# Routing of two expert layers moved into the per-batch chains, with a staggered write stage, in a four-layer transformer kernel

## The chip, the core and the metric

The kernel runs on one core of a Trainium2 chip. The engines named here are PE (matrix products, with PEld for its weight loads), DVE (vector operations), ACT (activations), POOL (GpSimd, which also issues the indirect transfers) and SP (which issues most plain transfers). DMA transfers go through queues of SP, ACT and POOL. The metric is the device time of one execution in microseconds (us).

## The reference, cut to what matters

Four layers, each a cross-attention and a feed-forward part with experts, on x of 4 batches x 512 tokens x 128 features. What the change touches is how tokens are assigned to expert slots in layers 0 and 2:

```python
# layer 0: one expert for each token, 8 experts, 128 slots each
logits = x @ w_switch + b_switch
routes = softmax(logits).argmax(-1)
oh = one_hot(routes)
pos = (cumsum(oh, axis=0) * oh).sum(-1) - 1
keep = pos < capacity                      # 128
buf[routes * capacity + pos] = x           # tokens kept
y = relu(buf_e @ w1 + b1) @ w2 + b2
out = where(keep, y[slot], x)

# layer 2: two experts for each token, 8 experts, 640 slots each
topv, topi = top_k(x @ w_g, 2)
mask = one_hot(topi.T)                     # all first choices, then all second
rank = cumsum(mask.reshape(2 * N, 8), axis=0) - 1
mask = mask * (rank < capacity)            # 640
# each kept (token, choice): gelu(x @ c_fc[e]) @ c_proj[e], weighted and summed
```

Slots are handed out in the order of tokens, first choices of all tokens before second choices. Which slot a token has does not show in the output; whether it has one does. Layer 1 has 16 experts on 16 soft slots a batch, between a "read" attention (slots look at tokens) and a "write" attention (tokens look at slots). Layer 3 computes all 8 experts on all tokens.

## The kernel before

Tokens lie in tiles of 128; a batch is four tiles (`NJ` = 4, `NT` = 16 in all), and X[g] holds batch g's rows. Work on a batch is written as a generator, a chain, that yields between its parts. `together(chains, skew)` (line 110) advances all running chains by one part in turn; chain i starts i x skew rounds late, and with skew 0 all go in lockstep. `queue` joins generators one after another. This gives the program order; a scheduler then fixes the order on each engine, and an engine works strictly in it.

The stages in order of time in the profile: layer 0's attention with the logits of `routed` (to about 140 us), layer 0's routing and experts in `l0_ffn` (to 184), layer 1's attention and read stage (to 252), layer 1's experts (to 276), the write stage with layer 2's attention and logits (to 341), layer 2's routing (to 357) and experts (to 460) in `l2_ffn`, layer 3's attention and gate (to 546), layer 3's experts (to the end).

Routing before is one block for all 2048 tokens, after the last batch's logits. `argmax` (line 579) finds the first largest logit as a one-hot tile of 128 x 128 (16 tiles x 8 experts); `without` (593) masks it for the second choice. `places` (597) counts tokens of each expert and tile with a product against ones (603), copies the counts on ACT (605), and adds a product with a triangle (608, ranks within a tile) to one with the counts of earlier tiles (611) and, for second choices, those of all first choices (610); `own` and `rank` (613 to 616) pick each token's rank. `tokens_of_slots` (620) turns ranks into a table from slots to tokens: rank modulo 128 as a one-hot 128 x 128 block `R` per tile (637), chunk number and token number in `th` (648), one product for each tile summed in PSUM (652), and a few small operations to `inv` (which token row to gather) and `to` (which row to scatter to). All of them are on DVE, with PE and ACT between.

In layer 0 the eight gathers (`xg`, 680, POOL) and the eight transpositions (712, PE, and copies 713, DVE) are all issued before the first expert. `hidden(e)` (732 to 739) makes the four hidden blocks, with two relus on DVE (737) and two on ACT (739); `outputs` (747, 749) follows for the expert before; each expert's rows are scattered (689, POOL) into `yd`. `combine` (763) reads yd back as `yg`, one transfer of 256 KB a batch on SP, and layer 1 adds it to X (457). Ahead of `l0_ffn` stand eight loads of 512 KB on SP's queue, `e_wg`, one weight of layer 1's experts (`halves`, 1197); the other, `e_w1` (in the profile `e_w`), follows during the experts, and `yg` lies behind its first loads in SP's queue.

The write stage (line 976) runs, for each batch, `write(g)` (block keys, 16-head attention on 16 slots, projection, add to X), then `attend2(g)` and `route2(g)`, the four chains in lockstep. `normed` makes the normalised rows, on DVE (223) or, where `act` is set, on ACT (219). Layer 3's chains and layer 1's read stage run with skew 2 (lines 1134 and 896).

Of the kernel before, what the change touches and what calls it, by code (L numbers as in the profile page):

```python
# [8 lines left out]
F32 = mybir.dt.float32  # L9
# [7 lines left out]
P = 128  # L17
# [28 lines left out]
_CST = [("ident", 128), ("ones", 128), ("tri", 128), ("before", 128), ("same", 128), ("vm8", 64),  # L46
        ("vm16", 32), ("vms", 64), ("hi32", 4), ("hi16", 8), ("selE", 128), ("hm2", 2), ("hm8", 8), ("hm16", 16), ("iota", 128), ("rev", 8),
        ("tile", 2 * NT), ("row", 1), ("spare0", NEXP), ("spare2", NCH2 * NEXP), ("chunks", NCH2), ("ctxT", 128)]
# [19 lines left out]
def tile_kernel(ctx: ExitStack, tc: tile.TileContext, I, out):  # L68
# [8 lines left out]
    rk = ctx.enter_context(tc.tile_pool(name="rk", bufs=1))  # L77

# [83 lines left out]
    for name in ("ones", "tri", "before", "same", "iota", "rev"):  # L162
        exact[name] = const.tile([P, C[name].shape[1]], BF16, tag=f"b_{name}", name=f"b_{name}")
        nc.gpsimd.tensor_copy(exact[name], C[name])
    ones, tri, before, same, iota, rev = exact.values()
# [334 lines left out]
    def l0_xattn(w):  # L500
        every = lambda r: bc(r, 1, NJ)

        def chain(g):
# [20 lines left out]
            hT = [l0.tile([P, S], F32, tag="hT", name="hT", bufs=16) for _ in range(4)]  # L524
# [26 lines left out]
    def routed(tag, w, bias=None, copies=()):  # L551
# [5 lines left out]
        def chain(g):  # L557
            xn[g] = yield from normed(X[g], "xn")
# [20 lines left out]
    def argmax(L, n=NT):  # L579

        m = rt.tile([P, n], F32, tag="m", name="m", bufs=2 * NT // n)
# [4 lines left out]
        w = rt.tile([P, n], F32, tag="w", name="w", bufs=2 * NT // n)  # L586
        nc.vector.tensor_reduce(w, at, AX.X, ALU.max)
        oh = rt.tile([P, n, NEXP], BF16, tag="oh", name="oh", bufs=2 * NT // n)
        nc.vector.tensor_tensor(oh, at, bc(w, 2, NEXP), ALU.is_equal)
        return m, oh  # L590

    def without(L, oh, n=NT):
# [4 lines left out]
    def places(ohs):  # L597

        sums, found = [], []
        for k, oh in enumerate(ohs):  # L600
            oh2 = oh.rearrange("p t e -> p (t e)")
            pt = psum()
            nc.tensor.matmul(pt[:, :P], lhsT=oh2, rhs=ones, start=True, stop=True)
            cs = rt.tile([P, P], BF16, tag="cs", name="cs", bufs=2)
            nc.scalar.copy(cs, pt[:, :P])
            sums.append(cs)
            pt = psum()
            nc.tensor.matmul(pt[:, :P], lhsT=tri, rhs=oh2, start=True, stop=False)
            for k0 in range(k):
                nc.tensor.matmul(pt[:, :P], lhsT=sums[k0], rhs=same, start=False, stop=False)  # L610
            nc.tensor.matmul(pt[:, :P], lhsT=cs, rhs=before, start=False, stop=True)
            own = rt.tile([P, NT, NEXP], F32, tag="own", name="own")
            nc.vector.tensor_tensor(own.rearrange("p t e -> p (t e)"), oh2, pt[:, :P], ALU.mult)
            rank = rt.tile([P, NT], F32, tag="rank", name="rank", bufs=2)
            nc.vector.tensor_reduce(rank, own, AX.X, ALU.add)
            nc.vector.tensor_scalar(rank, rank, -1.0, None, ALU.add)
            found.append(rank)
        return found

    def tokens_of_slots(ohs, ranks, cap, spare):  # L620
# [6 lines left out]
        pt = psum()  # L627
        for k, (oh, rank) in enumerate(zip(ohs, ranks)):
            ri = rt.tile([P, NT], I32, tag="ri", name="ri", bufs=2)
            nc.vector.tensor_copy(ri, rank)  # L630
            nc.vector.tensor_scalar(ri, ri, P - 1, None, ALU.bitwise_and)
            lo = rt.tile([P, NT], BF16, tag="lo", name="lo", bufs=2)
            nc.vector.tensor_copy(lo, ri)
            Rs = []
            for t0 in range(0, NT, NJ):
                R = wk.tile([P, NJ, P], BF16, tag="aT", name="R", bufs=B)
                nc.vector.tensor_tensor(R, bc(iota, 1, NJ), bc(lo[:, t0 : t0 + NJ], 2, P), ALU.is_equal)
                Rs.append(R)
                if t0 == 0:
                    hi = rt.tile([P, NT], F32, tag="hi", name="hi", bufs=2)  # L640
                    nc.vector.tensor_tensor(hi, rank, lo, ALU.subtract)
                    in_ = rt.tile([P, NT, nch], BF16, tag="in", name="in_", bufs=2)
                    nc.vector.tensor_tensor(in_, bc(hi, 2, nch), bc(C["chunks"][:, :nch], 1, NT), ALU.is_equal)
                    tk = rt.tile([P, NT, 2, NEXP], BF16, tag="tk", name="tk", bufs=2)
                    nc.vector.tensor_scalar(tk[:, :, 0, :], oh, C["row"], None, ALU.mult)
                    nc.vector.tensor_tensor(tk[:, :, 1, :], oh, bc(C["tile"][:, k * NT : (k + 1) * NT], 2, NEXP), ALU.mult)
                    th = rt.tile([P, NT, nch, 2 * NEXP], BF16, tag="th", name="th", bufs=2)
                    nc.vector.tensor_tensor(
                        th, bc(tk.rearrange("p t i e -> p t (i e)"), 2, nch), bc(in_, 3, 2 * NEXP), ALU.mult
                    )  # L650
            for t in range(NT):
                nc.tensor.matmul(
                    pt[:, : nch * 2 * NEXP],
                    lhsT=Rs[t // NJ][:, t % NJ, :],
                    rhs=th[:, t].rearrange("p c e -> p (c e)"),
                    start=k == 0 and t == 0,
                    stop=k == len(ohs) - 1 and t == NT - 1,
                )
        inv = rt.tile([P, nch, NEXP], I32, tag="inv", name="inv")
        got = rt.tile([P, nch, 2, NEXP], F32, tag="got", name="got")  # L660
        nc.vector.tensor_copy(got.rearrange("p c i e -> p (c i e)"), pt[:, : nch * 2 * NEXP])
        token = rt.tile([P, nch, NEXP], F32, tag="token", name="token")
        nc.vector.scalar_tensor_tensor(token, got[:, :, 1, :], float(P), got[:, :, 0, :], ALU.mult, ALU.add)
        row = rt.tile([P, nch, NEXP], F32, tag="row", name="row")
        nc.vector.tensor_scalar(row, token, -1.0, 0.0, ALU.add, ALU.max)
        if len(ohs) > 1:
            again = rt.tile([P, nch, NEXP], F32, tag="again", name="again")
            nc.vector.tensor_scalar(again, row, float(NTOK), float(-NTOK), ALU.is_ge, ALU.mult)
            nc.vector.tensor_tensor(inv, row, again, ALU.add)
        else:  # L670
            nc.vector.tensor_copy(inv, row)
        to = rt.tile([P, nch, NEXP], I32, tag="to", name="to")
        none = rt.tile([P, nch, NEXP], F32, tag="none", name="none")
        nc.vector.tensor_scalar(none, token, 0.0, None, ALU.is_equal)
        nc.vector.tensor_tensor(none, none, spare.rearrange("p (c e) -> p c e", c=nch), ALU.mult)
        nc.vector.tensor_tensor(to, row, none, ALU.add)
        return inv, to
# [39 lines left out]
    def l0_ffn(xd, yd, L):  # L717


        _, oh = argmax(L)  # L720
        (rank,) = places([oh])
        inv, to = tokens_of_slots([oh], [rank], L0_CAP, C["spare0"])
        b2 = ex.tile([P, NEXP, D], F32, tag="b2", name="b2")
        nc.scalar.dma_start(b2, I["f0_b2"].partition_broadcast(P))

        xTs = [expert_inputs(fetched(xd, inv, e, 0, 1, NEXP), NEXP) for e in range(NEXP)]

        def hidden(e):
            xT = xTs[e]
# [4 lines left out]
            for f in range(4):  # L734
# [3 lines left out]
                else:  # L738
                    nc.scalar.activation(hT[:, f, :], pt[:, f, :], AF.Relu, bias=b1)
# [96 lines left out]
    def l1_ffn(lw, dq, dv, cq, wg, before, after):  # L836
# [139 lines left out]
        together(queue(write(g), after(g)) for g in range(B))  # L976
# [25 lines left out]
    def l2_ffn(xd, yd, L, f2w1, f2w2, meanwhile):  # L1002
        m1, oh1 = argmax(L)
        m2, oh2 = argmax(without(L, oh1))
        ranks = places([oh1, oh2])

        d = rt.tile([P, NT], F32, tag="d", name="d")
        nc.gpsimd.tensor_tensor(d, m2, m1, ALU.subtract)
        nc.scalar.activation(d, d, AF.Exp)
        inv, to = tokens_of_slots([oh1, oh2], ranks, L2_CAP, C["spare2"])  # L1010
# [92 lines left out]
    def l3_ffn(xnT, logits, f3w1, f3w2, before, fetch):  # L1103
        gates = [None] * B

        def gate(g):
            L = logits[:, g * NJ : (g + 1) * NJ, :]
            m1, oh1 = argmax(L, NJ)
            m2, oh2 = argmax(without(L, oh1, NJ), NJ)
# [64 lines left out]
    for at in range(0, 2 * NTOK, S):  # L1174
        nc.sync.dma_start(yd2[at : at + S].rearrange("(j p) d -> p j d", p=P), zero)
    made = {}
# [229 lines left out]
```

## Time and profile before

| what | us |
| --- | --- |
| median of 14 executions | 677.61 (673.3 to 679.25) |
| the profiled execution, whole | 676.5 |
| its span in the profile | 674.7 |
| last logits of layer 0 to first gather | 140.41 to 149.83 |
| first hidden product of layer 0's experts | 161.66 |
| first rows back, layer 1 starts | 186.61 |
| first score product of the write stage | 276.2 |
| last logits of layer 2 to its first gather | 340.18 to 357.12 |

The granted PE clock was 0.852 over the span. In the views, each line of a timeline has start, duration, engine, line of the kernel, operation, output <- inputs, shape and count, and in brackets the engine's idle time before it with what ended it. Each line of the table by stretches has start:end and length, busy time (and instructions) of PE, PEld, DVE, ACT and POOL, the granted PE clock (1 is full), the mean share of the 16 DMA engines that was busy, and GB/s.

### The profile page before, as it was taken

The page shows a single profiled execution, that of the slowest core. Times are in us where ns is not written, and L with a number is a line of the kernel's source. Part 1 is how long each engine was busy: PE and PEld are TensorE (multiplying, and loading weights), DVE is VectorE, ACT ScalarE, POOL GpSimd, SP SyncE. Part 2 cuts the span into 40 slices and gives each one's busy share as a digit, 9 for nine tenths or more (in the row PEclk, how much of TensorE's full clock was granted, in tenths as well). Part 3 has the DMA queues.
Part 4 walks back from the last instruction along what each step waited for, and adds up shares of the span by engine and source line. Part 5 has one row for each costly group of instructions (what it writes and reads, how often), then busy time and mean ns, then how long its engine had stood idle before and what let it go on. Part 6 is the DMA issues. An engine that isn't in the chain of part 4 may idle for free.

```text
span 674.7 us, 8842 instructions
## 1 busy us (share of the span) xinstructions
PE 516.9 (77%) x3047; PEld 393.6 (58%) x3047; DVE 330.1 (49%) x1378; ACT 239.6 (36%) x539; POOL 163.9 (24%) x203
## 2 busy tenths in 40 slices
PE   3668988426678969787635999951799699999996
PEld 2557765325556543676523887840467557676765
DVE  4686555452377640367781322115767843333322
ACT  2354655300224731324211233221645333333342
POOL 4234234204512100100006777772100000000000
PEclk9979989855855988889675999995799869999999
DMA  9900001281390006300201112354000000000000
GB/s 325 305 29 18 17 16 53 59 309 32 132 291 0 1 0 236 139 2 1 63 1 39 56 52 50 54 175 140 0 1 1 1 0 2 17 0 17 1 17 16
DMA packets 42990, 44.97 MB, mean 67 GB/s; under 512 B 5161, under 2 KB 31026, under 8 KB 42818
## 3 DMA queue, kind: packets, MB, share of 16 engines
q1 hardware_dynamic: 39442, 36.20, 16.2%
q0 software_dynamic: 3072, 6.30, 3.6%
q10 hardware_dynamic: 432, 1.92, 0.7%
q8 instruction: 24, 0.39, 0.3%
q14 instruction: 20, 0.16, 0.1%
HBM read 34.97 MB, written 9.44 MB: 66 GB/s over the span
## 4 chain that ended last, share of the span: by engine, by line
PE 49%; DVE 11%; POOL 5%; DMA 5%; issue 5%; ACT 4%; SPq 1%; POOLq 0%; DVEq 0%; ACTq 0%
PE pt L1146 9%; PE pt L1151 9%; PE pt L1037 4%; PE pt L1045 4%; PE po L404 3%; PE pt L385 3%; POOL yd L689 3%; PE pt L233 3%; PE pt L916 2%; DMA yd<-ye,to 2%; PE pt L398 2%; PE pt L564 2%; POOL xg L680 1%; DVE st L192 1%; PE pt L452 1%
## 5 line engine op out<-in xcount | busy, mean ns | idle before, releaser
L1151 PEld LDWEIGHTS pt<-f3w,hT 128*128 128x128 f32 x512 | 66.1, 192 | 34.0 <-ACT hT L1147 19.0
L1161 DVE SCALAR_TENSOR_TENSOR x<-pt,gates,x 128x128 f32<-128x128 f32 x128 | 36.0, 345 | 84.2 <-PE pt L1151 84.2
L1147 ACT ACTIVATE hT<-pt,cols 128x512 f32<-128x512 f32 x64 | 44.0, 687 | 75.0 <-PE pt L1146 74.7
L1151 PE MATMUL pt<-f3w,hT 128*128 128x128 f32 x512 | 68.6, 277 | 0.9 <-ACT hT L1147 0.6
L1146 PE MATMUL pt<-xnT,f3w 128*128 128x512 f32 x128 | 68.0, 619 | 0.0
L233 PE MATMUL pt<-cst,xn 128*128 128x128 f32 x96 | 25.9, 366 | 42.1 <-ACT xn L219 22.9
L680 POOL DMA_INDIRECT xg<-xd,inv x48 | 46.1, 961 | 44.5 <-DMA e_wg<-in_e_wg 16.4
L1040 ACT ACTIVATE hT<-pt 128x384 f32<-128x384 f32 (+1 forms) x64 | 27.9, 437 | 73.6 <-PE pt L1037 72.1
L689 POOL DMA_INDIRECT yd<-ye,to x48 | 47.0, 979 | 25.6 <-DVE ye L749 13.1
L233 PEld LDWEIGHTS pt<-cst,xn 128*128 128x128 f32 x96 | 15.8, 170 | 53.8 <-ACT xn L219 27.8
L192 DVE BATCH_NORM_STATS2 st<-x 128x6 f32<-128x128 f32 x128 | 32.3, 270 | 23.7 <-POOL x L545 17.6
L1045 PEld LDWEIGHTS pt<-f2w,hT 128*128 128x128 f32 x320 | 39.6, 191 | 3.3
L1045 PE MATMUL pt<-f2w,hT 128*128 128x128 f32 x320 | 40.4, 279 | 0.0
L1037 PE MATMUL pt<-exT,f2w 128*128 128x256 f32 (+1 forms) x128 | 39.1, 449 | 1.0 <-DVE exT L713 1.0
L235 ACT COPY xnT<-pt 128x512 f32<-128x512 f32 x40 | 23.1, 585 | 43.0 <-PE pt L233 42.7
L1052 DVE COPY ye<-pt 128x384 f32<-128x384 f32 (+1 forms) x16 | 7.9, 491 | 57.5 <-PE pt L1045 37.5
L398 PE MATMUL pt<-cst,att 128*128 128x128 f32 x128 | 22.4, 301 | 12.6 <-ACT att L372 12.6
L372 ACT ACTIVATE att<-att 128x512 f32<-128x512 f32 x32 | 20.0, 631 | 27.7 <-DVE att L371 27.6
L1037 PEld LDWEIGHTS pt<-exT,f2w 128*128 128x128 f32 x128 | 23.8, 197 | 9.0 <-DVE exT L713 1.2
L385 PE MATMUL pt<-keys,xnT 128*128 128x256 f32 (+1 forms) x64 | 27.9, 543 | 0.9 <-ACT xnT L235 0.9
L370 DVE TENSOR_REDUCE mx<-pt 128x16 f32<-128x512 f32 (+1 forms) x32 | 21.7, 683 | 12.9 <-PE pt L385 12.7
L404 PEld LDWEIGHTS po<-v,aT 128*128 128x128 f32 x192 | 25.0, 201 | 4.9 <-issue 3.3
(297 smaller groups left out, 1030.5 us busy)
## 6 DMA issues: line engine op xcount, KB each, us to landing
e_wg<-in_e_wg SPq DMA_DIRECT2D x8, 512.0 KB, 7.5
e_w<-in_e_w SPq DMA_DIRECT2D x8, 512.0 KB, 7.1
yg<-yd SPq DMA_DIRECT2D x12, 256.0 KB, 3.6
f0w<-in_f_w SPq DMA_DIRECT2D x1, 2048.0 KB, 13.2
yd<-zero SPq DMA_DIRECT2D x8, 256.0 KB, 3.9
ew<-in_e_w SPq DMA_DIRECT2D x8, 256.0 KB, 3.7
xd<-xn SPq DMA_DIRECT2D x8, 256.0 KB, 2.2
f2w<-in_f_w SPq DMA_DIRECT2D x1, 2048.0 KB, 8.7
```

Of the source, the lines that this page charges most:

```text
L192: nc.vector.bn_stats(st[:p, j, :], src[:, j, :])
L233: nc.tensor.transpose(pt[:, j * P : (j + 1) * P], src[:, j, :], ident)
L385: nc.tensor.matmul(pt[:, j * nk : (j + 1) * nk], lhsT=xT[:, (j0 + j) * P : (j0 + j + 1) * P], rhs=keys, start=True, stop=True,)
L404: nc.tensor.matmul(po[:, k, :], lhsT=aT[:, k * P : (k + 1) * P], rhs=of(values[k % nch], cols + hpc, g), start=True, stop=True,)
L680: nc.gpsimd.indirect_dma_start(out=dst, out_offset=None, in_=table[:], in_offset=bass.IndirectOffsetOnAxis(ap=idx, axis=0))
L689: ins = nc.gpsimd.indirect_dma_start(out=table[:], out_offset=bass.IndirectOffsetOnAxis(ap=to[:, c, e : e + 1], axis=0), in_=y, in_offset=None
L1037: nc.tensor.matmul(pt[:, : m * P], lhsT=f2w1[:, e, f * P : (f + 1) * P], rhs=xT, start=True, stop=True)
L1045: nc.tensor.matmul(pt[:, c * D : (c + 1) * D], lhsT=hT[:, f, c * P : (c + 1) * P], rhs=f2w2[:, e, f, :], start=f == 0, stop=f == 3,)
L1146: nc.tensor.matmul(pt, lhsT=f3w1[:, e, f * P : (f + 1) * P], rhs=xnT[g], start=True, stop=True)
L1147: nc.scalar.activation(hT[:, f, :], pt, AF.Gelu, bias=col["f3_b1"][:, 2 * e + f : 2 * e + f + 1])
L1151: nc.tensor.matmul(pt[:, j, :], lhsT=hT[:, f, j * P : (j + 1) * P], rhs=f3w2[:, e, f, :], start=f == 0, stop=f == 1,)
L1161: nc.vector.scalar_tensor_tensor(xj, pt[:, j, :], ge, xj, ALU.mult, ALU.add)
```

## The change

1. Routing is made per batch. `argmax`, `places` and `tokens_of_slots` give way to `first_max` and `assigned(rt, logits, choices, cap, spare)`. `assigned` returns `chain(g)`, which is queued behind `route0(g)` and `route2(g)`, `finish()`, which makes `inv` and `to` after all batches, and `top`, the largest logits.
2. In the chain, counts of earlier batches are added by products with `same`; the triangle is strict, so that ranks begin at 0. `R` is made by one operation for each tile, comparing a constant row with a column of ranks; the products of each batch are added to a running sum `got`.
3. For layer 2, second choices no longer continue the count of the first. They are counted by themselves and take places from the back of the expert's 640 slots (a reversed row `back` and a reversed table of chunks); where a slot falls to both, the first choice has it.
4. In `l0_ffn`, each expert's transposition and copy stand just before its hidden product, and only its own gather is awaited.
5. The loads `e_wg` move from SP's queue before routing to ACT's queue, issued after the last relu of expert 4.
6. The write stage runs with skew 3. Layer 2's normalised rows are made on ACT (`act=True`).

Buffers move with it: `R` has its own, layer 0's hidden tiles have 12 instead of 16, and the right side of the memory holds `e_wg` and then layer 2's routing tiles.

```diff
-    def routed(tag, w, bias=None, copies=()):
+    def routed(tag, w, bias=None, copies=(), act=False):
...
-            xn[g] = yield from normed(X[g], "xn")
+            xn[g] = yield from normed(X[g], "xn", act=act)
...
+    def assigned(rt, logits, choices, cap, spare):
...
+        def chain(g):
+            oh = rt.tile([P, n, NEXP], BF16, tag="oh", name="oh", bufs=2)
+            L = logits[:, g * NJ : (g + 1) * NJ, :]
+            for k in range(choices):
+                ohk = oh[:, k * NJ : (k + 1) * NJ, :]
+                first_max(rt, top[k][:, g * NJ : (g + 1) * NJ], ohk, L)
+                if k + 1 < choices:
+                    L = without(rt, L, ohk)
+            flat = oh.rearrange("p t e -> p (t e)")
+            pt = psum()
+            nc.tensor.matmul(pt[:width, :P], lhsT=flat, rhs=ones, start=True, stop=True)
+            cs = rt.tile([P, P], BF16, tag=f"cs{g}", name="cs")
+            nc.scalar.copy(cs[:width], pt[:width, :P])
+            counts.append(cs)
...
+            yield
+
+            pt = psum()
+            nc.tensor.matmul(pt[:, :width], lhsT=tri, rhs=flat, start=True, stop=False)
+            for g0 in range(g):
+                nc.tensor.matmul(pt[:, :width], lhsT=counts[g0][:width], rhs=same[:width, :width], start=False, stop=False)
+            nc.tensor.matmul(pt[:, :width], lhsT=cs[:width], rhs=before[:width, :width], start=False, stop=True)
...
+            R = rt.tile([P, n, P], BF16, tag="R", name="R", bufs=2)
+            for t in range(n):
+                nc.vector.tensor_scalar(R[:, t, :], back if t >= NJ else iota, lo[:, t : t + 1], None, ALU.is_equal)
+            yield
...
+            if got:
+                nc.vector.tensor_tensor(flat, pt[:, : choices * m], got[-1].rearrange("p k c i e -> p (k c i e)"), ALU.add)
+            else:
+                nc.vector.tensor_copy(flat, pt[:, : choices * m])
+            got.append(now)
+            yield
...
-        xTs = [expert_inputs(fetched(xd, inv, e, 0, 1, NEXP), NEXP) for e in range(NEXP)]
+        xs = [fetched(xd, inv, e, 0, 1, NEXP) for e in range(NEXP)]
 
         def hidden(e):
-            xT = xTs[e]
+            xT = expert_inputs(xs[e], 3)
...
-                    nc.scalar.activation(hT[:, f, :], pt[:, f, :], AF.Relu, bias=b1)
+                    done = nc.scalar.activation(hT[:, f, :], pt[:, f, :], AF.Relu, bias=b1)
+            if e == NEXP // 2:
+                with tc.issue_after(done.ins):
+                    meanwhile()
...
-        together(queue(write(g), after(g)) for g in range(B))
+        after = then()
+        together([queue(write(g), after(g)) for g in range(B)], 3)
...
-            *(queue(attend0(g), route0(g)) for g in range(B)),
+            *(queue(attend0(g), route0(g), assign0(g)) for g in range(B)),
...
+    slots0 = finish0()
...
-        wg = halves("e_wg", gw, ("wga", "wgb"))
...
+        combine0 = l0_ffn(xd0, yd0, *slots0, lambda: wg.extend(halves("e_wg", gw, ("wga", "wgb"), nc.scalar)))
...
+    route2, _, _, L = routed(2, wide["w_g"], None, (xd2,), act=True)
...
+        return lambda g: queue(attend2(g), route2(g), made["assign2"](g))
```

More of the change, by code (lines that the diff above doesn't have):

```diff
@@ L523, in chain @@
             nc.gpsimd.tensor_tensor(z, z, every(w["rest"][:, 1]), ALU.add)
-            hT = [l0.tile([P, S], F32, tag="hT", name="hT", bufs=16) for _ in range(4)]
+            hT = [l0.tile([P, S], F32, tag="hT", name="hT", bufs=12) for _ in range(4)]
             for f in range(4):
@@ L620, in tokens_of_slots @@
-    def tokens_of_slots(ohs, ranks, cap, spare):
-        nch = cap // P
[L627 to L651, printed above, removed]
-                nc.tensor.matmul(
[L653 to L657, printed above, removed]
-                )
[L659 to L677, printed above, removed]
@@ L834, in l1_ffn_weights, with l1_ffn @@
         return dq, dv, cq
-    def l1_ffn(lw, dq, dv, cq, wg, before, after):
+    def l1_ffn(lw, dq, dv, cq, wg, before, then):
         sc = 1.0 / math.sqrt(8.0)
```

186 lines of the change are left out of this document (118 added, 68 removed).

## The prediction

> **What bounds the kernel now.** I read the page first, then a table of busy time cut at the stages that the change touches, then the timeline inside them, and last the DMA issues.
>
> ```profile
> PE 516.9 (77%) x3047; PEld 393.6 (58%) x3047; DVE 330.1 (49%) x1378; ACT 239.6 (36%) x539; POOL 163.9 (24%) x203
> ```
>
> PE is the busiest engine, but over the whole span. The change touches four stretches only (start:end, length, then busy us of PE, PEld, DVE, ACT and POOL, the granted clock, DMA share, GB/s), with a fifth for comparison:
>
> ```profile
> 133.00:150.00 17.00, 4.73 (x31) 3.41 (x31) 10.25 (x44) 1.26 (x4) 0.58 (x2) 0.50 0.85 308
> 150.00:162.00 12.00, 3.76 (x10) 1.88 (x11) 2.13 (x8) 0.00 (x0) 7.61 (x8) 0.50 0.15 44
> 162.00:184.00 22.00, 17.16 (x128) 16.78 (x127) 7.58 (x25) 5.87 (x16) 7.78 (x8) 0.81 0.28 97
> 276.00:341.00 65.00, 49.48 (x322) 44.37 (x320) 42.47 (x182) 22.59 (x54) 1.64 (x4) 0.82 0.10 31
> 341.00:357.00 16.00, 3.62 (x39) 2.69 (x39) 14.07 (x51) 2.03 (x4) 0.40 (x1) 0.62 0.00 0
> 460.00:546.00 86.00, 63.10 (x345) 46.33 (x346) 66.57 (x306) 36.92 (x85) 5.05 (x4) 0.80 0.09 25
> ```
>
> Line 1 is the end of layer 0's attention and its routing, line 2 the eight gathers and transpositions, line 3 its eight experts, line 4 the write stage with layer 2's attention in lockstep, line 5 layer 2's routing (DVE 14.07 of 16 us, PE nearly idle). Line 6 is layer 3's attention and gate: four chains already staggered, DVE 77% busy.
>
> In layer 0 the timeline gives the marks:
>
> ```profile
> 140.41 0.19 DVE L572 TENSOR_TENSOR logits<-pt,adds 128x32 f32<-128x32 f32 x1 [3.32 <-PE pt L564]
> 148.72 0.17 DVE L671 CAST inv<-row 128x8 int32<-128x8 f32 x1
> 149.83 1.17 POOL L680 DMA_INDIRECT xg<-xd,inv  x1 [16.41 <-DMA e_wg<-in_e_wg]
> 152.83 0.45 PE L712 MATMUL pt<-cst,xg 128*128 128x128 f32 x1 [4.76 <-DMA xg<-xd,inv]
> 161.66 3.64 PE L732 MATMUL pt<-exT,f0w 128*128 128x128 f32 x16
> 174.17 0.37 ACT L739 ACTIVATE hT<-pt,cols 128x128 f32<-128x128 f32 x1 [0.91 <-DVE hT L737]
> 179.97 0.97 POOL L689 DMA_INDIRECT yd<-ye,to  x1 [0.31 <-issue]
> 183.87 2.02 SPq L763 DMA_DIRECT2D yg<-yd  x4
> 186.61 0.69 DVE L457 TENSOR_TENSOR x<-yg,x 128x512 f32<-128x512 f32 x1 [7.12 <-DMA yg<-yd]
> ```
>
> The last batch's logits come at 140.4, the first gather at 149.8, its transposition at 152.8, yet the first hidden product at 161.7, behind all eight gathers; experts end with the last scatter at 180.0, and layer 1 starts at 186.6 when the rows are back. Layer 2's routing, and layer 3's logits for comparison:
>
> ```profile
> 340.18 0.19 DVE L570 COPY logits<-pt 128x32 f32<-128x32 f32 x1 [0.70 <-PE pt L564]
> 347.58 1.48 DVE L648 TENSOR_TENSOR th<-tk,in__3295 128x1280 bf16<-128x1280 bf16 x1
> 357.12 1.04 POOL L680 DMA_INDIRECT xg<-xd,inv  x1 [14.03 <-DVE to L676]
> ...
> 525.68 0.19 DVE L570 COPY logits<-pt 128x32 f32<-128x32 f32 x1 [0.78 <-PE pt L564]
> 543.34 0.19 DVE L570 COPY logits<-pt 128x32 f32<-128x32 f32 x1 [0.86 <-PE pt L564]
> ```
>
> ```profile
> e_wg<-in_e_wg SPq DMA_DIRECT2D x8, 512.0 KB, 7.5
> ```
>
> **Part 1, layer 0's routing in the chain.** Three batches are routed while later ones are normed and projected; only the last is left. Their DVE operations (some 20 each of 0.16 to 0.19 us) partly delay the last batch's logits: I take +1.0 us, bounds 0 and +3. After those logits come five first-maximum operations at 0.2 (layer 3's 128x32 rows take 0.16 to 0.19) = 1.0, the hop over PE and ACT for counts and ranks 1.1 (142.16 to 143.25 now), two 0.2 for the rank, four one-hot blocks at 0.2 = 0.8, the matmuls and sum 0.5, four closing operations 0.8, and 0.94 from the end of inv to the gather: 5.7 with the copy of the logits. Today it is 149.83 - 140.41 = 9.4. First gather: 149.8 + 1.0 - 3.7 = **147.1**.
>
> **Part 2, each expert on its own gather.** Transposition 3.0 after the gather as now, at 150.1, hidden product at about 151.0 instead of 161.7. But the transposition (0.45), its copy (0.29) and their hand-overs now sit in PE's order before each hidden product, so an expert costs 1.06 + 1.06 + 0.45 + about 0.2 = 2.75 instead of the 1.79 between scatters, and the first two run at the 0.50 clock. Gathers follow every 1.25 us and are no bound. Expert 4's relu ends near **164**, bounds 162 and 166 (now 173.3).
>
> **Part 3, e_wg on ACT's queue.** This takes a wait away and puts one in. On SP the eight 512 KB loads began at 139.8 and were over before the first expert. Now ACT issues them between the relus of expert 4 and expert 5. In the program's waits the seventh issue awaits the landing of the second, the eighth that of the fourth, since the loads share few semaphores. With landings of 6.8 to 8.8 us and 0.4 to 1.1 per issue, ACT stands 8 to 11 us, to 172 to 175. Behind it wait the relus of experts 5 to 7, and behind those DVE's outputs, the scatters on POOL, and yg on SP, which also lies behind four e_w1 loads with waits on e_wg landings. Then come one relu pair (0.9) and the rest of three experts (about 5): last scatter near 178.5 instead of 180.0. Then 8 + 4 loads and yg, 7.4 MB by 390 GB/s (the 2-us slices of this stretch reach 390 to 408) from 164, are through only at 183 at best, and yg, issued at 182.5, lands in 3 to 5 instead of 2.7: **186 to 187.5** against 186.6. Layer 0 nets **+0.5**, bounds -3 (issues short, loads overlap) and +4 (ACT held to 177).
>
> [...]
>
> **Part 4, the stagger of the write stage.** The first score product needs only batch 0's folded keys: 274.8 instead of 276.2, -1.4. DVE has 42.5 + 14.1 = 56.6 now; -4.5 (16 normalisations of 0.28 to ACT), -14.1 (old routing), +20 (four batches of 31 operations: 23 small ones, 0.12 apart where independent ones stand together and 0.20 where each waits for the last, eight one-hot blocks at 0.17, th at half of the 1.48 row: 4.9 to 6.7, I take 5.0), +1.5 (closing) = 59.5. It grows a little; what changes more is where it stands. The end is shorter: from the last logits to the gather 2.2 (choices) + 1.1 (hop) + 1.2 (ranks) + 2.1 (blocks, th) + 0.65 + 1.0 + 0.85 = 9.1 against 357.12 - 340.18 = 16.9, thus -7.8. But the last logits come later, because the front runs with one or two chains in flight and DVE's order puts it behind PE and ACT there, and because each batch's assignment stands before the next batch's logits. Following DVE's order instruction by instruction with the durations of the rows above, I get the first logits at 319, then steps of 11, 9.5 and 9.3 us: last logits at 349, gather at **359**, so **+2**. A check from layer 3: its logits step (543.34 - 525.68) / 3 = 5.9 with a gate of some 2.6 in each; with 5.0 for the assignment it is 10.9 if the gate stays in, 8.3 with the gate taken out. By 8.3 the gather comes at 319 + 25 + 9.1 = 353, by 10.9 at 361: -4 and +4, the walk between. I take the walk, since in line 4 PE is the busier engine (49.5 against 42.5) and DVE will wait for it more than in line 6, and keep -8 to +6 for the range.
>
> A one-hot block is costed by the nearest row, L645, 0.25 us with 0.17 to the next start. [...] No row of before shows this form.
>
> Eight clearing operations on POOL in the write stage now stand between two of its multiplications and await the last product of batch 3's first attention. They are small (0.14 to 0.6 us); hidden by the next chain's DVE work, else about 1 us. Moving the normalisation to ACT is hidden too: ACT is busy 22.6 of 65 us; if it were not, 16 times 0.42 (ACT's three normalisations at L219 that take 1.25 in the chain of waits) = 6.7 less the 4.5 saved. Everything after the first gather of layer 2 keeps its order on every engine: 0.
>
> **Sum.** 676.5 + 0.5 + 2.0 = 679.0 for an execution like the profiled one. That one lies 1.1 under the median of 677.6, so I predict **680.1**.
>
> **The rivals.** (a) Faster: the stagger works as in layer 3, at the DVE share of 77%: 56.5 to 59.5 by 0.77 is 73 to 77 us from 274.8, gather at 348 to 352, -7; with layer 0 at -0.5 it gives **670** (667 if layer 0 gains its 3). For it: line 6 is the same kind of work, and lockstep leaves DVE at 65% now. Against: the assignment chains go over PE and ACT twice each and stand in a row at the end. It decides if layer 2's first gather comes before 355. (b) The parts cancel: write stage -2 or layer 0 -2.5, **677.5**. For it: a first-logits mark that is 4 us earlier than my walk is enough. Against: both terms would have to miss in the same direction. (c) ACT's pause is longer and yg waits among the loads: +4 in layer 0, +4 in the write stage, **686**. For it: three waits of SP on e_wg landings ahead of yg. Against: the loads are together only 6 MB. (d) The code is placed otherwise than the text of the change says and the last batch's logits are not followed at once by its choices: then layer 0's routing saves nothing, and 3.7 is lost, **684**; the order of instructions speaks against it.
>
> **How the numbers follow.** Forecast 0.38 (679.7 to 683), (a) 0.33, (b) 0.14, (c) 0.11, (d) 0.04. Differences within 0.3%, about 2 us, cannot be told from none. Faster: (a) = 0.33. Same: (b) = 0.14. Slower: forecast, (c) and (d) = 0.53. The range leaves out the part of (a) below 667 (both stages at their lower bounds would be 667) and the end of (c) above 687: 667 to 687. The likeliest's own range is 679.7 to 683.
>
> **What would show it.** Part 1: first layer-0 gather 146 to 148.5. Part 2: first hidden product before 153, scatters 2.5 to 3 us apart. Part 3: a gap of 8 us or more on ACT after expert 4, with e_wg issues in it; yg's rows used near 187. Part 4: logits of layer 2 at steps of 9 to 11 us, last logits to gather about 9, first layer-2 gather at 357 to 361 (after taking off layer 0's shift). It is wrong if ACT issues the loads without pausing, or if the logits step like layer 3's.

## The result, and the profile after

The changed kernel takes 694.73 us (median of 10 executions, 688.37 to 697.39) against 677.45 before: a ratio of 1.0241, 95% interval 1.0216 to 1.0265. The ratios compare the means of the fast executions, so they are not the quotients of the medians. The profiled execution took 697.3 us, 2.6 above its median.

The page of the changed kernel, busy time by engine over the span:

```profile
span 695.5 us, 9008 instructions
...
PE 534.6 (77%) x3073; PEld 404.7 (58%) x3073; DVE 339.0 (49%) x1484; ACT 247.0 (36%) x560; POOL 163.8 (24%) x204
```

DVE has 8.9 us more work; PE is busy for 17.7 us more, with only 26 more products. Where the 20.8 us between the spans lie is read from marks. The changed kernel's timeline in layer 0 (start, duration, engine, line, operation, idle before):

```profile
148.33 0.19 DVE L574 TENSOR_TENSOR logits<-pt,adds 128x32 f32<-128x32 f32 x1 [3.31 <-PE pt L566]
152.64 0.17 DVE L704 CAST inv<-row 128x8 int32<-128x8 f32 x1
153.75 1.18 POOL L718 DMA_INDIRECT xg<-xd,inv  x1 [13.61 <-DVE to L712]
157.59 2.08 PE L766 MATMUL pt<-exT,f0w 128*128 128x128 f32 x8 [0.38 <-DVE exT L751]
172.45 8.35 ACTq L1235 DMA_DIRECT2D e_wg<-in_e_wg  x8
180.90 1.67 ACT L773 ACTIVATE hT<-pt,cols 128x128 f32<-128x128 f32 x6 [8.09 <-DMA e_wg<-in_e_wg]
185.75 0.97 POOL L727 DMA_INDIRECT yd<-ye,to  x1 [0.31 <-issue]
191.05 2.02 SPq L800 DMA_DIRECT2D yg<-yd  x4
195.48 0.69 DVE L459 TENSOR_TENSOR x<-yg,x 128x512 f32<-128x512 f32 x1 [11.22 <-DMA yg<-yd]
```

And the first score product of the write stage, layer 2's logits and its first gather:

```profile
287.99 1.13 PE L387 MATMUL pt<-keysc,xnT 128*128 128x256 f32 x4 [0.46 <-ACT keysc L1006]
...
332.82 0.19 DVE L572 COPY logits<-pt 128x32 f32<-128x32 f32 x1
346.15 0.19 DVE L572 COPY logits<-pt 128x32 f32<-128x32 f32 x1 [0.25 <-PE pt L566]
357.77 0.19 DVE L572 COPY logits<-pt 128x32 f32<-128x32 f32 x1 [0.25 <-PE pt L566]
368.63 0.19 DVE L572 COPY logits<-pt 128x32 f32<-128x32 f32 x1 [0.25 <-PE pt L566]
378.03 1.04 POOL L718 DMA_INDIRECT xg<-xd,inv  x1 [7.35 <-DVE other L709]
```

Taking the same marks from both traces, each stretch can be set against its own (us; first gather to last scatter is from start to start):

| stretch | before | after | difference |
| --- | --- | --- | --- |
| start to layer 0's last logits | 140.4 | 148.3 | +7.9 |
| last logits to first gather | 9.4 | 5.4 | -4.0 |
| first gather to last scatter | 30.1 | 32.0 | +1.9 |
| last scatter to rows back (first use of yg) | 6.6 | 9.7 | +3.1 |
| rows back to first score product of the write stage | 89.6 | 92.5 | +2.9 |
| first score product to last logits of layer 2 | 64.0 | 80.6 | +16.6 |
| last logits to first gather of layer 2 | 16.9 | 9.4 | -7.5 |
| first gather of layer 2 to the end | 317.6 | 317.5 | -0.1 |

Both routing tails became shorter, as the change intends (-4.0, -7.5). The work that went into the chains delays the last logits by more (+7.9, +16.6).

### The profile page after: what moved, and what is told of

The parts are those of the page before. It is cut to its first block, busy times and chain, and to the rows that moved or that the text cites. A ratio compares the mean times of both kernels' runs of the same rounds, so it can differ in the third digit from the quotient of the medians.

```text
span 695.5 us, 9008 instructions
## 1 busy us (share of the span) xinstructions
PE 534.6 (77%) x3073; PEld 404.7 (58%) x3073; DVE 339.0 (49%) x1484; ACT 247.0 (36%) x560; POOL 163.8 (24%) x204
## 3 DMA queue, kind: packets, MB, share of 16 engines
q1 hardware_dynamic: 37266, 32.01, 15.4%
## 4 chain that ended last, share of the span: by engine, by line
PE 57%; DVE 16%; issue 8%; DMA 8%; POOL 6%; ACT 4%; SPq 0%; POOLq 0%; DVEq 0%; ACTq 0%
PE pt L1187 8%; PE pt L1182 8%; PE po L406 4%; PE pt L235 4%; PE pt L387 4%; PE pt L247 3%; PE pt L1071 3%; PE pt L1079 3%; POOL yd L727 3%; DMA yd<-ye,to 2%; DVE st L194 2%; PE pt L566 2%; PE pt L400 2%; DMA xg<-xd,inv 2%; PE pt L891 2%
## 5 line engine op out<-in xcount | busy, mean ns | idle before, releaser
L1187 PEld LDWEIGHTS pt<-f3w,hT 128*128 128x128 f32 x512 | 65.6, 191 | 33.3 <-ACT hT L1183 19.0
L194 DVE BATCH_NORM_STATS2 st<-x 128x6 f32<-128x128 f32 x128 | 32.4, 272 | 14.7 <-POOL x L547 8.8
L235 PEld LDWEIGHTS pt<-cst,xn 128*128 128x128 f32 x96 | 15.7, 177 | 40.3 <-ACT xn L221 26.9
L374 ACT ACTIVATE att<-att 128x512 f32<-128x512 f32 x32 | 20.2, 632 | 30.2 <-DVE att L373 29.8
L221 ACT ACTIVATE xn<-x,c,r 128x128 f32<-128x128 f32 x64 | 26.7, 483 | 10.5 <-DVE c L218 7.2
L400 PE MATMUL pt<-cst,att 128*128 128x128 f32 x128 | 22.0, 295 | 10.9 <-ACT att L374 10.8
L199 ACT ACTIVATE y<-v 128x4 f32<-128x4 f32 (+1 forms) x45 | 9.1, 203 | 58.6 <-DVE v L197 58.4
```

What stands on the lines that cost most here:

```text
L194: nc.vector.bn_stats(st[:p, j, :], src[:, j, :])
L235: nc.tensor.transpose(pt[:, j * P : (j + 1) * P], src[:, j, :], ident)
L400: nc.tensor.transpose(pt[:, k * P : (k + 1) * P], e[:, k * P : (k + 1) * P], ident)
L1187: nc.tensor.matmul(pt[:, j, :], lhsT=hT[:, f, j * P : (j + 1) * P], rhs=f3w2[:, e, f, :], start=f == 0, stop=f == 1,)
```

## The experiments

Runs went to several chips. The kernel before took 703.6 us on the chip of e1, e3, e4 and e7, 700.6 on that of e5_skew1, e6, e9 and e10, and 677.9 on that of e5_skew2, e11, e12 and e13, so times are compared as ratios to the before of the same chip. Up to layer 2's first gather the chips agree: e4_own_gather, which differs from before in layer 0's experts alone, has its marks within 0.7 us of before's everywhere up to 356 us, the stretch it changes aside. Stretches as in the table above:

| run | logits to gather | gather to scatter | scatter to rows | rows to score | score to last logits | logits to gather 2 | ratio (95%) |
| --- | --- | --- | --- | --- | --- | --- | --- |
| before | 9.4 | 30.1 | 6.6 | 89.6 | 64.0 | 16.9 | 1 |
| after | 5.4 | 32.0 | 9.7 | 92.5 | 80.6 | 9.4 | 1.0241 (1.0216 to 1.0265) |
| e3_assign0_after | 8.6 | 33.3 | 9.4 | 86.0 | 79.3 | 9.4 | 1.0195 (1.0051 to 1.034) |
| e7_yield | 5.4 | 33.3 | 9.7 | 85.2 | 78.6 | 9.8 | 1.0195 (1.0095 to 1.0294) |
| e1_wg_sp | 5.4 | 30.6 | 6.9 | 86.0 | 79.4 | 9.4 | 1.0154 (1.0056 to 1.0252) |
| e10_wg_last | 5.4 | 29.9 | 10.3 | 94.2 | 80.6 | 9.4 | 1.0277 (1.023 to 1.0324) |
| e4_own_gather | 9.4 | 29.5 | 7.0 | 89.6 | 63.9 | 16.9 | 0.9991 (0.9955 to 1.0027) |
| e6_assign2_after | 5.4 | 33.6 | 9.4 | 91.6 | 70.9 | 19.9 | 1.0279 (1.0211 to 1.0347) |
| e5_skew1 | 5.4 | 33.6 | 9.4 | 87.4 | 63.8 | 12.4 | 1.0077 (1.0044 to 1.011) |
| e5_skew2 | 5.4 | 32.0 | 9.8 | 92.6 | 71.4 | 9.8 | 1.0127 (1.0103 to 1.0152) |
| e9_l0_mended | 5.4 | 25.7 | 6.8 | 89.9 | 62.8 | 16.4 | 0.9875 (0.983 to 0.992) |
| e11_mended_skew1 | 5.4 | 24.2 | 7.1 | 92.5 | 58.3 | 15.7 | 0.9724 (0.9697 to 0.9752) |
| e12_mended_skew1_dve | 5.4 | 24.3 | 6.7 | 84.3 | 59.8 | 15.4 | 0.9762 (0.9738 to 0.9786) |
| e13_after_again | 5.4 | 31.9 | 9.8 | 92.5 | 80.7 | 9.4 | 1.0233 (1.021 to 1.0256) |

### Why layer 0's last logits are late

PE of the changed kernel around batch 0's assignment, from the timeline, and then DVE:

```profile
119.46 0.29 PE L624 MATMUL pt<-b_ones,oh 128*32 128x128 bf16 x1 [3.99 <-DVE oh L590]
119.67 6.45 PE L529 MATMUL pt<-xnT,w 128*128 128x512 f32 x8
126.07 0.18 PE L639 MATMUL pt<-b_before,cs 32*128 32x32 bf16 x1
```
```profile
126.29 0.19 DVE L641 TENSOR_TENSOR own<-oh,pt 128x32 f32<-128x32 bf16 x1 [5.73 <-PE pt L639]
```

The counts product (L624) needs the one-hot tile that DVE makes by five small operations among others. It stands in PE's order ahead of eight hidden products of another batch (L529), and PE idles 3.99 us in front of it. Those products then take 6.45 us; in the kernel before they took 3.70. The table by stretches (start:end and length, busy us and instructions by engine, granted PE clock, DMA share, GB/s) shows why, first for after, in the idle time and in the products:

```profile
115.50:119.46 3.96, 0.00 (x1) 0.01 (x1) 3.96 (x23) 1.00 (x3) 2.53 (x2) 0.87 0.00 0
119.67:126.12 6.45, 6.45 (x11) 2.67 (x10) 0.79 (x6) 3.74 (x8) 1.96 (x2) 0.57 0.30 81
```

and for before in the same products:

```profile
113.57:117.27 3.70, 3.70 (x10) 1.74 (x11) 3.63 (x20) 0.99 (x3) 1.95 (x2) 1.00 0.00 0
```

The clock granted was 0.87 over the 3.96 us of idling and 0.57 in the products after it, instead of the 1.00 in before's. That the idling lowered the clock is the author's reading of these rows. Then DVE stands 5.73 us at `own`, whose product is behind those eight, with the next batch's normalisation behind it. Two experiments test this: one takes the assignments out of the chains, the other leaves them in but lets other chains' PE work go first.

```diff
-            *(queue(attend0(g), route0(g), assign0(g)) for g in range(B)),
+            *(queue(attend0(g), route0(g)) for g in range(B)),
...
+    together([assign0(g) for g in range(B)], 1)
     slots0 = finish0()
```

> The changed kernel with layer 0's assignment taken out of the batch chains and run after them, one round apart. Theory (PE stands at the counts product of an earlier batch and the ready hidden products behind it are late): the last logits come 5 us earlier, at 143 instead of 148.3 in the profile; but four assignments then lie between them and the first gather, 9 to 11 us instead of 5.4, so the time is within 2 us of the changed kernel's, 693 to 696. Rival (the logits are late because DVE has more to do, some 40 small operations at 0.1): the last logits come 2 to 3 us earlier and the time is 2 to 4 us above the changed kernel's.

The last logits came at 142.4 instead of 148.3, 5.9 earlier, and 8.6 us lay between them and the gather instead of 5.4. Of the 5.9 us, 0.7 were there at the first logits already (116.2 against 117.0), before any assignment runs. The other 5.2 are the theory's 5 us and not the rival's 2 to 3. The ratio's interval is too wide to tell the time from the changed kernel's.

```diff
             flat = oh.rearrange("p t e -> p (t e)")
+            yield
             pt = psum()
             nc.tensor.matmul(pt[:width, :P], lhsT=flat, rhs=ones, start=True, stop=True)
```

> The changed kernel with one more yield in the assignment chain, between the choices on DVE and the counts product on PE, so that other chains' PE work is put ahead of the product that waits. Nothing is added or taken away. Theory (PE waiting for the one-hot tile, 14.7 us in four waits in the write stage and some 6 in layer 0, is on the path): 5 to 9 us less, 686 to 690. Rival (the assignments' DVE work itself is what takes the time, 63.3 us busy instead of 56.5): within 2 us of the changed kernel, 693 to 697.

In layer 0 the theory held. With one yield the logits came at 141.8 and the first gather at 147.2, with the same operations. Not all of these 6.5 us are the yield's: 2.7 were there at the first logits already (114.3 against 117.0), as in e1_wg_sp, which has the changed kernel's instructions up to that point and its first logits at 114.1. From the first to the last logits it is 27.6 us instead of 31.4 (before 26.0), so the yield is worth 3.8. PE's waits for the one-hot tile between 100 and 150 us fell from 10.1 to 5.4 us. The eight hidden products are fast again, 3.70 us at a granted clock of 1.00, and stand ahead of the counts product, which no longer waits (PE's timeline of this run):

```profile
113.45 3.70 PE L529 MATMUL pt<-xnT,w 128*128 128x512 f32 x8 [0.67 <-ACT xnT L237]
117.08 0.23 PE L625 MATMUL pt<-b_ones,oh 128*32 128x128 bf16 x1
```

In the write stage it missed: from score product to layer-2 gather 88.5 instead of 90.0, though PE's wait for the one-hot tile fell from 14.7 to 9.1. Another cause rules there.

### The pause on ACT

```diff
-    wg = []
+    wg = halves("e_wg", gw, ("wga", "wgb"))
     with tc.tile_pool(name="ex0", bufs=1) as ex:
-        combine0 = l0_ffn(xd0, yd0, *slots0, lambda: wg.extend(halves("e_wg", gw, ("wga", "wgb"), nc.scalar)))
+        combine0 = l0_ffn(xd0, yd0, *slots0, lambda: None)
```

> The changed kernel with one part undone: the eight e_wg loads go back to SP's queue ahead of layer 0's experts. Theory (ACT's 8.35 us of load issues hold the relus of experts 5 to 7, and yg then meets the loads): experts go on at 2.8 us each, so the last scatter comes some 29 us after the first gather instead of 32.0, and the rows are back 6.6 us after it instead of 9.7: 6 us less in all, 688 to 689. Rival 1 (the pause is hidden, yg waits for the bus either way): 0 to 2 us less, 693 to 695. Rival 2 (the whole pause and yg's delay come back): 11 less, 683 to 684.

Gather to scatter 30.6 instead of 32.0 and scatter to rows 6.9 instead of 9.7: 4.2 us, of the 6 expected. The ratio fell from 1.0241 to 1.0154, with a wide interval. The 1.4 us at the scatters hide two things. On SP's queue the loads are still under way when the first gather is issued (405 GB/s from 150 to 152 us), and PE waits longer for its rows (e1_wg_sp, then the changed kernel):

```profile
155.03 0.45 PE L750 MATMUL pt<-cst,xg 128*128 128x128 f32 x1 [5.82 <-DMA xg<-xd,inv]
```
```profile
156.76 0.45 PE L750 MATMUL pt<-cst,xg 128*128 128x128 f32 x1 [4.77 <-DMA xg<-xd,inv]
```

That is 4.1 us after the gather instead of 3.0: moving the loads saved 1.1 us there. From the first hidden product to the last scatter the changed kernel takes 28.2 us and e1_wg_sp 25.7, so the pause costs 2.5. That is far less than the 8.09 us for which ACT stood still, since the outputs that had waited followed close together (the last three scatters 1.3 us apart, at 183.20, 184.47 and 185.75). The larger part was yg's lateness behind the loads, 2.8 us.

```diff
-            if e == NEXP // 2:
+            if e == NEXP - 1:
```

> The changed kernel with the e_wg loads on ACT's queue issued after the last expert's relus instead of expert 4's: no relu is behind them, but they begin some 8 us later and meet yg fully. Theory (both the pause on ACT and the meeting with yg cost): first gather to last scatter falls from 32.0 to 29 to 30 us, but last scatter to rows back grows from 9.7 to 12 to 15: 0 to 3 us above the changed kernel. Rival (only the pause costs): 29 to 30 and 9 to 10: 2 to 3 us less than the changed kernel.

29.9 and 10.3: 2.1 less and 0.6 more. So the pause costs 2.1 us by this run, 2.5 by the one before; the loads keep yg back also here, though less than the 12 to 15 expected. The ratio of 1.0277 is not below the changed kernel's; in this run rows back to score product took 94.2.

### Each expert on its own gather

```diff
-        xTs = [expert_inputs(fetched(xd, inv, e, 0, 1, NEXP), NEXP) for e in range(NEXP)]
+        xs = [fetched(xd, inv, e, 0, 1, NEXP) for e in range(NEXP)]
 
         def hidden(e):
-            xT = xTs[e]
+            xT = expert_inputs(xs[e], 3)
```

> The kernel before with one part of the change alone: each expert's transposition stands before its own hidden product. Theory (the earlier start is paid back by 2.8 us an expert instead of 1.79, as the changed kernel's trace has it): last scatter 29 us after the first gather instead of 30.1, so 1 us less than before, 676 to 677. Rival (the start at 154 instead of 161.7 is kept to the end): 7 us less, 670. Second rival (slower experts lose more than the start gives): 3 us more, 680.

The first hidden product came at 153.3 instead of 161.7, but the last scatter only 0.6 us nearer to the first gather (29.5 against 30.1), and the ratio is 0.9991. The start is paid back at 2.84 us an expert. PE's timeline of the changed kernel shows one expert: products, then a transposition, then a wait for its copy on DVE in front of the next hidden product, each time.

```profile
165.10 1.06 PE L784 MATMUL pt<-f0w,hT 128*128 128x128 f32 x8
165.99 0.27 PE L750 MATMUL pt<-cst,xg 128*128 128x128 f32 x1
166.89 1.16 PE L766 MATMUL pt<-exT,f0w 128*128 128x128 f32 x8 [0.62 <-DVE exT L751]
167.88 1.06 PE L784 MATMUL pt<-f0w,hT 128*128 128x128 f32 x8
```

### The write stage

Its two changes, the stagger and the assignments in the chains, were taken apart.

```diff
-        return lambda g: queue(attend2(g), route2(g), made["assign2"](g))
+        return lambda g: queue(attend2(g), route2(g))
...
     finish2, top2 = made["places2"]
+    together([made["assign2"](g) for g in range(B)], 1)
```

> The changed kernel with the write stage staggered by 3, but layer 2's assignments run after it, one round apart, instead of in the chains. Theory (the stagger by 3 alone costs): the last logits come 70 us or later after the first score product (before 64.0, changed kernel 80.6), and the tail of four assignments takes 22 to 26 us: 92 to 98 in all, 2 to 8 us above the changed kernel. Rival (the assignments in the chains are what delays the logits, the stagger is free): last logits at 62 to 66, tail 22 to 26, 84 to 90 in all, 0 to 6 us below the changed kernel.

Last logits 70.9 us after the first score product, gather 19.9 later: 90.8, against 90.0 with the assignments in the chains. The logits are 6.9 later than in lockstep, so the rival, by which the stagger by 3 is free, is out; and the assignments add 9.7 to the logits inside the chains and save 10.5 at the end. The tail was shorter than expected, and the sum lies below the theory's 92 to 98.

```diff
-        together([queue(write(g), after(g)) for g in range(B)], 3)
+        together([queue(write(g), after(g)) for g in range(B)], 1)
```

> The changed kernel with the write stage staggered by 1 instead of 3; the assignments stay in the chains. Theory (with 3 rounds between them the batches end one by one, each alone, so that PE and DVE take turns): the four logits come close together again, and first score product to first layer-2 gather falls from 90.0 to 78 to 82 us (before: 80.9), 8 to 11 us less than the changed kernel, that is 1.008 to 1.014 of before. Rival (the assignment in the chain, 6.8 us more of DVE work and two turns over PE a batch, is what costs): 86 to 89 us, at most 3 us less than the changed kernel.

63.8 + 12.4 = 76.2, below before's 80.9 and 13.8 below the changed kernel's, although all the assignment work is in the chains. That is better than the theory's 78 to 82. The ratio falls to 1.0077. The rival is out. Lockstep with the assignments in the chains was not run.

```diff
-        together([queue(write(g), after(g)) for g in range(B)], 3)
+        together([queue(write(g), after(g)) for g in range(B)], 2)
```

> The changed kernel with the write stage staggered by 2. Theory (the length of the thin end, where one batch runs alone, sets the time): between the staggers of 1 (76.2 us from first score product to layer-2 gather) and 3 (88.5 to 90.0), 81 to 85 us. Rival (a special meeting of waits at 3 alone): 75 to 78.

71.4 + 9.8 = 81.2, between the two and at the low end of what was expected. The stretches from first score product to layer-2 gather, with staggers of 1, 2 and 3 (one kernel each):

```profile
282.20:358.30 76.10, 55.03 (x376) 47.28 (x376) 61.52 (x303) 31.92 (x77) 3.72 (x15) 0.80 0.11 36
```
```profile
288.10:369.30 81.20, 58.84 (x376) 49.04 (x376) 62.28 (x303) 31.50 (x77) 3.69 (x15) 0.76 0.09 31
```
```profile
288.00:378.00 90.00, 60.25 (x376) 49.45 (x376) 63.31 (x303) 31.84 (x77) 3.74 (x15) 0.77 0.09 29
...
332.80:378.00 45.20, 22.78 (x122) 17.12 (x120) 32.67 (x193) 12.51 (x33) 1.03 (x3) 0.58 0.07 18
```

The instructions are the same (303 on DVE, 376 on PE) and DVE's work nearly so, 61.5 to 63.3 us. Its share falls from 81% to 77% and 70%. The last line is the second half of the stagger by 3, from the first logits on: PE is busy for half the time, at a clock of 0.58. Each batch's end runs nearly alone there, DVE and PE in turns (PE's timeline, an excerpt):

```profile
332.62 0.60 PE L235 MATMUL pt<-cst,x 128*128 128x128 f32 x4
337.29 0.32 PE L624 MATMUL pt<-b_ones,oh 128*64 128x128 bf16 x1 [4.06 <-DVE oh L590]
```

### Putting the parts together

Layer 0's part alone on the kernel before, with the three faults mended: the yield, e_wg on SP, and each transposition issued one expert ahead:

```diff
+        xTs = [expert_inputs(xs[0], 3)]
+
         def hidden(e):
-            xT = expert_inputs(xs[e], 3)
+            xT = xTs[e]
...
             hT = hidden(e)
+            if e + 1 < NEXP:
+                xTs.append(expert_inputs(xs[e + 1], 3))
             if last is not None:
                 outputs(e - 1, last)
```

> The kernel before with layer 0's part of the change alone, mended in three places: the extra yield before the counts product, e_wg on SP's queue ahead of the experts as before, and each expert's transposition issued one expert ahead. Write stage and layer 2's routing are as before. Theory: first gather 2.6 us earlier than before (as in the run with the extra yield), last scatter 25 to 27 us after it instead of 30.1, rows back 6.6 to 7 after it: 5 to 8 us less than before, a ratio of 0.989 to 0.993. Rival (the experts are held by gathers, half clock and POOL): 2 to 3 us less, 0.996.

Gather to scatter 25.7, scatter to rows 6.8, ratio 0.9875. Against e4, which has the transpositions in line, the scatters gain 3.8 us. Issuing the transpositions one ahead is worth more, 5.6 us: 20.1 us from the first hidden product to the last scatter instead of 25.7. The first hidden product, however, came 5.6 us after the gather and not 3.8, with the loads on SP's queue still under way there (369 GB/s from 152 to 154 us). The first gather came at 150.8, not 147.2: its first batch's logits were at 117.8 against 114.3 in e7, and from there on the two agree to 0.1 us.

The changed kernel with the same three, and the stagger by 1:

> The changed kernel with all that helped in the earlier runs: the extra yield before the counts product in both layers, e_wg on SP ahead of the experts, each transposition one expert ahead, and the write stage staggered by 1. Theory (the gains are in different stages and add up): first gather to last scatter 25 to 27 us, last scatter to rows back 6.6 to 7, first score product to layer-2 gather 74 to 77: 11 to 15 us less than before, a ratio of 0.978 to 0.985. Rival (the extra yield spoils the stagger by 1, or a gain upstream is lost in waits of layer 1): 0.986 to 0.992, no better than the kernel with layer 0 alone mended.

660.79 us against 677.93, a ratio of 0.9724 (0.9697 to 0.9752), better than expected: the gains add up, and 58.3 + 15.7 = 74.0 from score product to gather. This version beats both kernels. Its stage from score product to gather is the shortest of all at a granted clock of 0.74, lower than the 0.77 of the stagger by 3:

```profile
273.60:347.50 73.90, 59.25 (x376) 49.95 (x376) 59.59 (x303) 32.03 (x77) 3.77 (x16) 0.74 0.10 34
```

So the clock alone does not explain what the stagger by 3 costs.

One more run took one part out of this kernel:

```diff
-    route2, _, _, L = routed(2, wide["w_g"], None, (xd2,), act=True)
+    route2, _, _, L = routed(2, wide["w_g"], None, (xd2,))
```

> The same kernel with layer 2's normalised rows made on DVE again. If the move to ACT matters, the write stage is 2 to 4.5 us longer (16 operations of 0.28 on a DVE that is the busier engine there). If it is hidden, as predicted, within 1 us either way.

59.8 + 15.4 = 75.2 against 74.0, 1.2 longer; the medians are 660.86 and 660.79. The move to ACT is worth about 1 us at most, and by the medians nothing that can be told.

> The changed kernel itself once more, beside the others on their chip, to see which marks of its profile repeat. Theory (the first 2.5 us by 70 us into the run, and part of the 92.5 us from rows back to first score product, are the granted clock's): last logits of layer 0 at 145 to 146 and 86 to 90 us. Rival (they belong to the change): 148 and 92. The ratio to before should be 1.022 to 1.027 again.

148.2 and 92.5 came again, and 1.0233. By this run alone the rival would stand. But e11 and e12 have the same instructions in the same order up to the write stage, and their last logits are at 144.2 and 141.9, and 92.5 and 84.3 from rows back to score product. The clock differs; 20 us of layer 1 in e11 and then the same place in e12:

```profile
200.00:220.00 20.00, 17.58 (x60) 12.09 (x59) 12.79 (x59) 9.51 (x26) 3.91 (x4) 0.50 0.00 0
```
```profile
197.30:217.30 20.00, 16.53 (x88) 11.48 (x87) 17.18 (x73) 14.41 (x39) 5.04 (x5) 0.90 0.00 1
```

60 products at a clock of 0.50 against 88 at 0.90 in the same 20 us. So the same instructions took 8.2 us more in e11. The 2.6 us at the first logits go with the clock as well: from 35 to 70 us the changed kernel had 0.83 and e1_wg_sp, with the same instructions up to the first logits, 0.90 (before: 0.90).

```profile
35.00:70.00 35.00, 26.55 (x152) 23.32 (x151) 24.74 (x103) 14.46 (x36) 12.40 (x17) 0.83 0.11 30
```
```profile
35.00:70.00 35.00, 25.34 (x161) 21.60 (x160) 26.80 (x111) 15.93 (x40) 13.21 (x18) 0.90 0.13 36
```

One kernel varies in this too: two executions of e11, of 657.06 and 666.22 us, had clocks of 0.863 and 0.843 over the span. So of the changed kernel's +7.9 and +2.9 some 2.6 and up to all of the second are not the change's own work. What decides when the clock rises stays open.

## Why the prediction was wrong

It said slower, by 2.5 us; it was 17.3 by the medians and 20.8 between the profiled executions, outside the range. The 18.3 us between 2.5 and 20.8, step by step:

- **Part 1, the delay of the last logits** (+1.0, bounds 0 and +3): +7.9. This is the step that failed. It counted the added operations on DVE and not where their products stand in PE's order: 5.4 came from PE standing before the counts product, the granted clock of 0.57 after it, and DVE standing before `own` (31.4 us from the first to the last logits against 26.0). With the yield 1.6 of these are left, near the predicted 1.0. The other 2.6 were there at the first logits (117.0 against 114.4), before any added routing, at a lower granted clock. The routing tail itself (5.7) was right: 5.4. Miss 6.6 together.
- **Part 2** held: first hidden product 3.8 after the gather (predicted 3.9), 2.84 an expert (2.75). Expert 4's relus ended 19.1 us after the gather, 2.2 later than the predicted 16.9.
- **Part 3** held in its mechanism: ACT's pause 8.09 to 8.35 (8 to 11), gather to scatter 32.0 (31.4), scatter to rows 9.7 (8.6 by its own net). Miss 1.7. Its reading that the loads of before began at 139.8 was wrong (three were issued from 133.4, five from 138.2), but its sum does not use it. In e1, with the loads out of yg's way, the rows were back 6.9 us after the last scatter, 2.8 sooner; in e10, with the loads later on ACT's queue, they stayed late, at 10.3.
- **Layer 1 and the start of the write stage** (-1.4): +2.9. The 1.4 is in the trace (the shift of PE's work falls from 13.2 to 11.8 us over the last products before the stage), but 4.3 us more were lost in layer 1, on the same work, at a granted clock of 0.72 over the stretch against 0.75. That the clock is the cause is argued from this and from e11 and e12, not tested. Miss 4.3, not foreseen at all; with the 2.6 of part 1 it makes 6.9 of the 18.3 us that go with the clock and not with a step of the sum.
- **Part 4, the steps between logits** (11, 9.5 and 9.3): 13.3, 11.6 and 10.9. The term was mis-sized by 6.0. The first logits (44.2 predicted after the first score product, 44.8 measured) and the tail (9.1, 9.4) were nearly right. DVE's work grew to 63.3, not 59.5, so the 5.0 us for a batch's assignment, near the lower of its bounds of 4.9 and 6.7, was too little; a one-hot block itself cost what was taken (0.25 us, 0.41 for two in a row). And the walk used the durations of before, while from the second logits on the granted clock was 0.50: eight products of L454 that took 1.15 us at 340.98, at a clock of 1.00, took 2.07 at 352.72. These misses add up to 6.9. From first score product to gather the miss is 5.8, because the prediction's terms, 319 + 29.8 + 9.1, end at 357.9 and it wrote 359.
- **Everything after layer 2's first gather at 0**: -0.1.

6.6 + 1.7 + 4.3 + 5.8 - 0.1 = 18.3. Rival (a) was wrong for the stagger by 3, but its DVE share was right for another: it took layer 3's 77%, layer 3 runs with a stagger of 2, and the changed kernel with a stagger of 2 has 77%. It takes 81 us where that rival's upper end was 77, since DVE's work there is 62.3 us and not 59.5.

## What to carry to other kernels

A small operation that is moved into a chain is not priced by its own time alone: ask on which engine its consumer stands in line, and what ready work is queued behind it; one more yield ahead of that consumer gave back 3.8 us here, nearly the 4.0 that the shorter routing tail saved. Of the staggers of 1, 2 and 3 the smallest was the best, since the last chain's end runs alone for its length: with the stagger by 3, PE was busy for 14.8 of the 31.9 us from the second logits to layer 2's first gather, at a granted clock of 0.50. A wait taken away from the start of a loop helps only if the loop's period stays (in e4 the first hidden product came 8.4 us sooner, the last scatter 0.6 nearer to the first gather); issue the new step one round ahead (5.6 us in e9).

## What was not expected of the hardware

- The same instructions in layer 1 took 84.3 and 92.5 us in two kernels on one chip, at granted PE clocks of 0.90 and 0.50 over the 20 us shown. In the row at 0.50 PE was busy for 17.58 of 20 us, and for 15.28 of the 19 us before it, also at 0.50: being busy did not raise the clock there. The profile names no cause.
- After 3.96 us of idle PE, products that took 3.70 us at a clock of 1.00 took 6.45 at 0.57, 2.75 us more, some 70% of the wait's own length. In e7, after 0.67 us of waiting, they took 3.70 at 1.00. That the wait is the cause is the author's reading.
- On two of the chips the kernels took 340 to 346 us from layer 2's first gather to the end instead of the 317 to 318 of the others. In e9's trace there, DVE waited 42 us in four waits in layer 2's experts for something that the profile calls remote (the line below: who waits, for what, us, times, longest). In the changed kernel's own trace there is no such wait. The cause is open.

```profile
DVE ye L1188 <- remote: 42.2, 4, 16.3
```
